# A causal convolution over eight sequences: its first sequence run ahead on its own, with idle products on TensorE and a causal matrix built without its zero columns

## The chip, the cores and the metric

The kernel runs on one core of a Trainium2 chip. The core has TensorE (PE in the profile, with its weight loads as PEld), VectorE (DVE), ScalarE (ACT), GpSimd (POOL) and SyncE (SP). Each of them takes its own instructions in order, and they wait for one another through semaphores. DMA transfers are issued from the queues of SP, ACT and POOL. The metric is the time of one execution on the device in microseconds; lower is better. A profiled execution has a time of its own, and within it a span from the first to the last instruction of the core.

## The reference

Four layers work on x of shape (8, 512, 128): a causal convolution, an FP4 feed-forward block, a test-time-training attention and a mixture of experts. Only the first is touched. For each of 8 sequences, with 16 heads of 8 channels and 31 taps, it computes:

```python
x = x + _L0_attn_ref(_layernorm(x, axis=-1), ...)

def _L0_attn_ref(x, W_pe, b_pe, stt_energy, W_fc, gamma, beta):
    residual = x
    avg = jnp.cumsum(x, axis=1) / jnp.arange(1, l + 1, dtype=x.dtype)[None, :, None]
    ci = avg.reshape(b, l, H, d).transpose(0, 2, 1, 3).reshape(b * H, l, d)
    pc = ci @ W_pe + b_pe
    dyn, gate = (pc[..., :K], pc[..., K:])
    energy = stt + jax.nn.sigmoid(gate) * dyn
    w = jax.nn.softmax(energy, axis=-1)
    ...
    for kk in range(K):
        out = out + w[:, :, kk:kk + 1] * padded[:, kk:kk + l, :]
    ...
    v = conv_loc @ W_fc.T + residual
    v = (v - mu) / jnp.sqrt(var + EPS) * gamma + beta
    return v
```

So each position needs the running mean of the normalised input, a gate and a tap value for each of 31 offsets, a softmax over the offsets, the weighted sum of the 31 last means, a projection and a second normalisation.

## The kernel before

`sequence_conv` holds the layer. It keeps channels in the 128 partitions and the 512 positions in the free dimension; the 31 taps go in four groups g of eight (16 heads x 8 taps = 128 partitions). Before any sequence it prepares constants: `inv` (1/t along 512 columns, by an iota on POOL and a reciprocal on DVE, L174 and L175), the causal matrix `tri` (four selects of 128 x 512 from `inv` on POOL, L190), the block weights `wbig` (eight multiplications on POOL, L214, behind a memset at L210), the biases, and the transposed projection `wfc_t`.

A sequence b goes through these steps, each a small function:

- `norm0` and `scaled` (L274): statistics on DVE, a root, then four scalings on ACT that write `xn`. The root is a Sqrt on ACT for the first two sequences and a chain of 13 short DVE instructions (`rsqrt`, L85 to L93) for 2 to 4 and for 5 to 7.
- `means` (L285): four matrix products of `xn` with `tri`, a copy of the result to `avg` on ACT (L288), and on SP one transfer to DRAM (`far`, L291) and eight back (`base`, L294), which spread the shifted means over the partitions.
- `gates` and `taps` (L300): for each g one matrix product for the gate, a Tanh and a linear step on ACT (L309, L310), and one product for the tap. Both write the two buffers of the pool `ps_e`.
- `energy` (L325 to L331): two DVE instructions for each g; the second keeps the running maximum `top`.
- `turn_top`, `greatest` (L341), `turn_greatest`: transposes on TensorE, a maximum on DVE, a copy on ACT, transposes back. `less` (L351) subtracts the maximum.
- `weigh` (L362, L364): seven exponentials on ACT.
- `shared` (L402) and `product` (L411): the products of weights and shifted means, two channels of eight on POOL and six on DVE for g of 0 to 2, all eight on DVE for g = 3. `add_up` (L420) sums them on TensorE.
- `part_sums`, `sums`, `invert`, `turn_inverse`: the softmax's denominator, over TensorE, ACT (`dn`, L375; `rw`, L386; `rbs`, L393) and DVE (L384).
- `scale_down` (L427), `project` (L432, L433), `norm1`, `finish` (L451 to L456): scaling, projection plus residual into a single-buffered PSUM pool `ps_p`, second normalisation, and the addition to x. The root of `norm1` runs on POOL (L130 to L138), on DVE for the last sequence.
- `add_beta` (L460): one POOL instruction that adds beta to x.

The order on each engine is written out by hand: `vec`, `ten`, `act` and `gp` are `Line` objects that chain an instruction behind the one given to them before. What is not given to a `Line` is put in place by the framework's scheduler. The loop at L496 works on three sequences at once: the products of b, the energies of b+1 and the gates of b+2, with the projection of b-1. The code ahead of the loop (L463 to L495) brings sequences 0, 1 and 2 to that state together. After the loop the buffers of the later layers are cleared and their weights loaded, all queued on SP.

## Time and profile before

| What | us |
|---|---|
| Median of 4 runs (lowest to highest) | 1301.51 (1300.51 to 1302.74) |
| The profiled execution | 1304.43 |
| Its span | 1302.7 |
| Busy in the span: PE, DVE, POOL, ACT | 1106.8, 771.6, 743.3, 489.7 |
| Mean granted TensorE clock | 0.939 of full speed |
| First `avg` copy of the convolution (L288) | 17.57 to 18.16 |
| First `product` of sequences 0, 1, 2, 3 (L411) | 44.55, 70.11, 96.87, 123.21 |
| Last `product` of the stage (L411) | 236.25 |
| x of the last sequence done (L456) | 253.43 |

Times in the trace are counted from the start of the span. A line of a timeline gives the start, the time from there to the end, the engine, the line of the kernel, the operation, what it writes and reads with the shapes, how many instructions were put together, and in brackets how long the engine was idle before and what released it. A product of two float32 operands appears as two records on TensorE (x8 stands for four). In the convolution the first product of one sequence follows that of the one before by about 26.3 us.

### The profile page before, as it was taken

The numbers are of one execution on the slowest core, as the hardware profiler recorded it, in microseconds if no ns is written. First come the engines' busy times: TensorE is split into PE (matmuls) and PEld (weight loads), VectorE is DVE, ScalarE is ACT, GpSimd is POOL, SyncE is SP. The second block draws the span as 40 slices with busy tenths as digits, with TensorE's granted clock in tenths as the row PEclk, the third lists the DMA queues.
The fourth block names the chain that finished last, engine by engine and source line by source line (L and its number), as shares of the span: only waits on it lengthen the run. The fifth ranks groups of instructions, "written<-read, shape, count | busy, mean of one in ns | idle before, by whom it ended". The sixth has DMA issues, their size and how long they took to land.

```text
span 1302.7 us, 15384 instructions
## 1 busy us (share of the span) xinstructions
PE 1106.8 (85%) x5219; PEld 659.6 (51%) x5219; DVE 771.6 (59%) x1769; ACT 489.7 (38%) x1001; POOL 743.3 (57%) x724
## 2 busy tenths in 40 slices
PE   5899997357877899999989999999899775499992
PEld 2343432135656445555565554555666444387772
DVE  7899999788985544444454444444556556033254
ACT  4556545166556422222243222222433122234331
POOL 4357656545554878888804887888103344355453
PEclk9899999878998899999999999999999886699997
DMA  5224327750000000000000000000000010212267
GB/s 157 77 77 124 106 77 238 278 172 1 1 1 1 1 1 1 1 1 1 1 1 1 1 1 1 1 1 1 1 1 21 29 33 30 62 51 70 64 178 207
DMA packets 66894, 67.26 MB, mean 52 GB/s; under 512 B 6927, under 2 KB 48734, under 8 KB 66816
## 3 DMA queue, kind: packets, MB, share of 16 engines
q1 hardware_dynamic: 59296, 56.57, 14.8%
q0 software_dynamic: 4608, 8.43, 2.1%
q10 hardware_dynamic: 2912, 1.29, 0.4%
q8 instruction: 41, 0.67, 0.2%
q14 instruction: 37, 0.30, 0.1%
HBM read 40.00 MB, written 27.13 MB: 52 GB/s over the span
## 4 chain that ended last, share of the span: by engine, by line
issue 66%; PE 9%; DMA 2%; POOL 1%; SPq 1%; DVE 0%; POOLq 0%; ACT 0%; DVEq 0%
PE ph L1470 4%; PE po L1483 4%; POOL own L1497 1%; DMA w<-in_L_ffn_W 1%; POOL res L1497 1%; PE tp L1455 1%; DMA own<-ye,tok 1%; DMA y<-own 1%; DMA L_ffn_bg<-in_L_ffn_bg 0%; DMA xe<-rows 0%; SPq L653 0%; SPq L759 0%; SPq L59 0%; DVE xt L1458 0%; SPq L1444 0%
## 5 line engine op out<-in xcount | busy, mean ns | idle before, releaser
L1141 POOL TENSOR_TENSOR ds<-sw,s 128x512 f32<-128x512 f32 x64 | 81.7, 1276 | 89.0 <-DVE sw L1136 89.0
L1371 POOL DMA_INDIRECT rows<-xr,slot x64 | 62.6, 977 | 106.1 <-DVE rs L93 55.5
L1143 POOL TENSOR_TENSOR ds<-ds,s 128x512 f32<-128x512 f32 x64 | 110.2, 1722 | 5.0
L1134 ACT COPY b<-pb 128x512 f32<-128x512 f32 x64 | 37.5, 586 | 163.0 <-PE pb L1130 156.4
L1497 POOL DMA_INDIRECT res<-ye,xe x60 | 58.5, 974 | 68.0 <-DVE ye L1495 29.7
L1138 DVE TENSOR_TENSOR h<-sw,b 128x512 f32<-128x512 f32 x64 | 51.7, 808 | 73.0 <-ACT b L1134 72.6
L1473 ACT ACTIVATE ht<-ph,b 128x512 f32<-128x512 f32 (+2 forms) x100 | 56.2, 589 | 94.3 <-PE ph L1470 75.4
L402 POOL TENSOR_TENSOR pr<-base,en 128x512 f32<-128x512 f32 x48 | 72.7, 1544 | 32.4 <-ACT en L364 32.3
L1144 POOL TENSOR_TENSOR ds<-ds,b 128x512 f32<-128x512 f32 x64 | 82.5, 1289 | 5.0
L1142 POOL TENSOR_TENSOR ds<-sw,ds 128x512 f32<-128x512 f32 x64 | 82.4, 1288 | 5.0
L1166 PEld LDWEIGHTS pp<-proj,ht 128*128 128x128 f32 x512 | 67.1, 191 | 30.8 <-issue 29.4
L411 DVE TENSOR_TENSOR pr<-base,w 128x3072 f32<-128x3072 f32 x24 | 79.7, 3320 | 1.7 <-ACT w L362 1.7
L1483 PE MATMUL po<-w,ht 128*128 128x128 f32 (+1 forms) x640 | 77.6, 278 | 0.3 <-ACT ht L1473 0.3
L1470 PE MATMUL ph<-xt,w 128*128 128x512 f32 (+2 forms) x200 | 74.1, 516 | 3.4 <-DVE xt L1458 3.4
L1136 DVE TENSOR_TENSOR sw<-pa,s 128x512 f32<-128x512 f32 x64 | 44.3, 692 | 54.5 <-ACT s L1132 54.5
L1161 ACT COPY ht<-pt 128x512 f32<-128x512 f32 x64 | 37.5, 586 | 103.3 <-PE pt L1159 103.3
L1483 PEld LDWEIGHTS po<-w,ht 128*128 128x128 f32 (+1 forms) x640 | 74.1, 188 | 1.3 <-ACT ht L1473 0.5
L1176 PE MATMUL ph<-proj_t,dpt 128*128 128x512 f32 x128 | 71.7, 642 | 0.4 <-ACT dpt L1174 0.4
L1178 DVE TENSOR_TENSOR db<-ph,sw 128x512 f32<-128x512 f32 x64 | 44.2, 691 | 45.5 <-PE ph L1176 45.5
L420 PE MATMUL cv<-pr,sel 128*32 128x512 f32 x512 | 61.8, 611 | 9.7 <-DVE pr L411 9.2
L1128 PE MATMUL pa<-gate,kt 128*128 128x512 f32 x128 | 67.7, 611 | 2.5 <-ACT b L1134 2.4
L1166 PE MATMUL pp<-proj,ht 128*128 128x128 f32 x512 | 67.6, 275 | 0.0
(327 smaller groups left out, 2590.2 us busy)
## 6 DMA issues: line engine op xcount, KB each, us to landing
base<-far SPq DMA_DIRECT2D x64, 268.0 KB
rows<-empty SPq DMA_DIRECT2D x1, 5005.0 KB
res<-zero SPq DMA_DIRECT2D x1, 4096.0 KB
own<-zero SPq DMA_DIRECT2D x2, 2048.0 KB
w<-in_L_ffn_W SPq DMA_DIRECT2D x16, 256.0 KB
y<-res SPq DMA_DIRECT2D x16, 256.0 KB
xe<-rows SPq DMA_DIRECT2D x7, 585.0 KB
y<-own SPq DMA_DIRECT2D x12, 256.0 KB
```

The source lines that it names most:

```text
L402: gp(nc.gpsimd.tensor_tensor(pr[:, d, :], s["base"][:, d, at], s["en"][:, g, :], ALU.mult))
L411: vec(nc.vector.tensor_tensor(s["pr"][g][:, :nv, :], s["base"][:, :nv, at], w.to_broadcast([P, nv, L]), ALU.mult))
L1128: nc.tensor.matmul(pa, ki, gate, start=True, stop=True)
L1141: nc.gpsimd.tensor_tensor(ds, sw, s, ALU.mult)
L1142: nc.gpsimd.tensor_tensor(ds, sw, ds, ALU.subtract)
L1143: nc.gpsimd.tensor_tensor(ds, ds, s, ALU.add)
L1144: nc.gpsimd.tensor_tensor(ds, ds, b, ALU.mult)
L1166: nc.tensor.matmul(pp, ht[:, c * P : (c + 1) * P], proj[:, c, :], start=(c == 0), stop=(c == NF - 1))
L1176: nc.tensor.matmul(ph, dpt, proj_t, start=True, stop=True)
L1470: ten(nc.tensor.matmul(ph[:, :n], self.w1[:, e, c * P : (c + 1) * P], xt[:, :n], start=True, stop=True))
L1483: ten(nc.tensor.matmul(po[:m, i - lo, :], ht[:, c, (i - lo) * P : (i - lo) * P + m], self.w2[:, e, c, :], start=(c == 0), stop=(c == NF - ...
L1497: sc = nc.gpsimd.indirect_dma_start(out=(self.slots.own[own - 1] if own else self.slots.res)[:, :], out_offset=bass.IndirectOffsetOnAxis(a ...
```

## The change

Part of it is about constants. `inv` is made by TensorE: an iota of 128 x 4 and a reciprocal of that (`by_t`), four products with the identity that spread it over the columns, and a DVE copy from PSUM. Behind those four, TensorE gets 14 products of the identity with itself (`busy`), whose result nobody reads. The selects for `tri` take only the columns from j x 128 on (512, 384, 256 and 128). The `wbig` products, the copy to `by_k` and `half` move from POOL to DVE, `wbig` as s within g. A Sqrt of a constant is run early on ACT, and the loads of `wrep`, the biases and `wfc` get places in ACT's line.

The rest is about order. The roots of sequences 0 and 1 are taken one by one, and the later ones by `roots`, a generator of 14 DVE instructions of which the caller places each. Sequence 0's gates write four PSUM buffers of other pools (`ps_w` and `ps_c`), one gate and one tap by turns. Sequence 0 is brought up to its first products before sequence 1's means are formed; the loop's body for b = 0 is written out ahead of the loop with sequences 1 and 2 filled in, and the loop starts at 1. `add_beta` is now in POOL's line, behind `shared` of its sequence in the loop. The means of sequences 1 and 2 are accumulated in the pool `ps_p`. The lines of the matrix products for the means are the same as before.

```diff
+    BUSY = 14
...
+        act(nc.scalar.activation(warm, cx.eps[1e-5], AF.Sqrt))
...
         inv = wp.tile([P, L], F32, tag="inv", name="inv")
-        nc.gpsimd.iota(inv, [[1, L]], base=1, channel_multiplier=0, allow_small_or_imprecise_dtypes=True)
-        vec(nc.vector.reciprocal(inv, inv))
+        by_t = wp.tile([P, G], F32, tag="by_t", name="by_t")
+        nc.gpsimd.iota(by_t, [[P, G]], base=1, channel_multiplier=1, allow_small_or_imprecise_dtypes=True)
+        vec(nc.vector.reciprocal(by_t, by_t))
+        pi = ps_c.tile([P, G, P], F32, tag="c", name="pi")
+        for j in range(G):
+            ten(nc.tensor.matmul(
+                pi[:, j, :], by_t[:, j : j + 1].to_broadcast([P, P]), cx.ident, start=True, stop=True
+            ))
+        busy = ps_p.tile([P, P], F32, tag="p", name="busy")
+        for _ in range(BUSY):
+            ten(nc.tensor.matmul(busy, cx.ident, cx.ident, start=True, stop=True))
+        vec(nc.vector.tensor_copy(inv, flat(pi)))
...
+                gp(nc.gpsimd.affine_select(
+                    out=tri[:, j, j * P :], in_=inv[:, j * P :], pattern=[[1, L - j * P]], compare_op=ALU.is_ge,
+                    fill=0.0, base=0, channel_multiplier=-1,
+                ))
...
+        stats0(0, 1)
+        root(0)
+        offset(0, 1)
+        scaled(0)
+        vec(nc.vector.tensor_copy(by_k.rearrange("h k s g -> h s g k"), rows.rearrange("h s (g k) -> h s g k", k=KK)))
+        act(nc.scalar.dma_start(
+            out=bias.rearrange("p s g -> p (s g)"), in_=by_k.rearrange("h k s g -> h (k s g)")
+        ))
+        for g in range(NGR):
+            for s in (1, 0):
+                n = min(KK, KC - KK * g)
+                vec(nc.vector.tensor_tensor(
+                    wbig[:, s, g, :, :n],
...
+        stats0(1, 2)
+        root(1)
+        offset(1, 2)
+        act(nc.scalar.activation(warm, cx.eps[1e-5], AF.Tanh))
+        wfc = wp.tile([P, D], F32, tag="wfc", name="wfc")
+        act(nc.scalar.dma_start(out=wfc, in_=ins["L0_attn_W_fc"]))
...
         seq = {0: means(0)}
-        gates(seq[0], 0)
+        stats0(2, 3)
+        half = wp.tile([P, NGR], F32, tag="half", name="half")
+        vec(nc.vector.tensor_scalar(half, bias[:, 1, :], 0.5, None, ALU.mult))
+        stats0(3, 5)
+        cur = seq[0]
+        for g, place in enumerate(((ps_w, "w0"), (ps_w, "w1"), (ps_w, "w2"), (ps_c, "c"))):
+            gate(cur, g, place)
+            tap(cur, g)
+            energy(cur, g)
         scaled(1)
...
+        turn_top(cur)
+        steps = roots(2, 5)
+        for _ in range(5):
+            next(steps)
+        greatest(cur)
+        turn_greatest(cur)
+        for _ in steps:
+            pass
+        less(cur)
+        weigh(cur, 0, 1)
+        nxt = seq[1] = means(1, ps_p, "p")
+        values(nxt, 0)
+        weigh(cur, 1, NGR)
+
+        shared(cur)
+        product(cur, 0)
+        part_sums(cur)
+        sums(cur)
+        for g in (0, 1):
+            energy(nxt, g)
+        values(nxt, 1)
+        product(cur, 1)
+        scaled(2)
+        then = seq[2] = means(2, ps_p, "p")
+        add_up(cur, 0)
         for g in (2, 3):
-            energy(seq[0], g)
...
+            energy(nxt, g)
+        invert(cur)
+        turn_top(nxt)
+        gates(then, 0)
+        stats0(5, B)
+        greatest(nxt)
...
+        less(nxt)
+        weigh(nxt, 0, 1)
+        seq[3] = means(3)
+        weigh(nxt, 1, NGR)
+        for _ in roots(5, B):
+            pass
+        product(cur, 3)
+        add_up(cur, 3)
+        for b in range(1, B):
```

## The prediction

> **What bounds the kernel now.** I read first the page's busy shares in 40 slices (32.6 us each). They show where VectorE (DVE) sets the pace.

> ```profile
> PE   5899997357877899999989999999899775499992
> DVE  7899999788985544444454444444556556033254
> PEclk9899999878998899999999999999999886699997
> ```

> The conv stage is the first seven to eight slices. DVE stands at 9 there, except in the first two, and the granted clock dips in the second. Everything after slice 8 issues the same instructions in the same order in both kernels, so only the first 253 us can change.

> Then the busy time by windows (columns: window, its length, then PE, PEld, DVE, ACT, POOL busy with counts, clock, DMA share, GB/s):

> ```profile
> 10.00:20.00 10.00, 5.96 (x12) 3.01 (x12) 8.13 (x39) 4.23 (x8) 4.06 (x10) 1.00 0.18 57
> 20.00:30.00 10.00, 9.00 (x25) 3.85 (x25) 5.66 (x8) 6.87 (x14) 1.91 (x3) 1.00 0.78 215
> 40.00:50.00 10.00, 9.24 (x21) 3.38 (x20) 8.29 (x6) 7.76 (x13) 4.56 (x6) 0.78 0.25 73
> 90.00:100.00 10.00, 9.66 (x44) 3.56 (x36) 10.00 (x4) 6.87 (x11) 4.56 (x5) 1.00 0.13 40
> ```

> From 60 us on DVE is full; before that it is not. What can be won is how early the full stretch begins. Its marker is the first `product` (L411) of sequence 1, at 70.11 in the trace. The timeline of the start:

> ```profile
> 7.14 1.28 ACT L268 ACT_TABLE_LOAD   x1 [7.14 <-DVE mv L257]
> 9.00 3.60 DVE L270 SCALAR_TENSOR_TENSOR off<-mv,rs 128x8 f32<-128x8 f32 x1
> 9.64 2.94 POOL L214 TENSOR_TENSOR wbig<-wrep,mask_h 128x128 f32<-128x128 f32 x8
> 13.27 4.25 PE L285 MATMUL av<-tri,xn 128*128 128x512 f32 x8 [13.27 <-ACT xn L274]
> 17.57 0.59 ACT L288 COPY avg<-av 128x512 f32<-128x512 f32 x1 [1.77 <-PE av L285]
> 26.67 2.32 PE L285 MATMUL av<-tri,xn 128*128 128x512 f32 x8
> 27.91 0.75 DVE L331 SCALAR_TENSOR_TENSOR top<-en,bias,top 128x512 f32<-128x512 f32 x1
> 40.61 2.28 DVE L351 TENSOR_TENSOR en<-en,mb 128x2048 f32<-128x2048 f32 x1
> 44.55 3.36 DVE L411 TENSOR_TENSOR pr<-base,w 128x3072 f32<-128x3072 f32 x1 [1.67 <-ACT w L362]
> ```

> The 0.17 us `off` takes 3.60, ending as POOL's run of `wbig` ends. The first means take 4.25 on a cold TensorE, 2.32 later. Between the last `top` of sequence 0 (28.66) and its `less` (40.61) stand statistics and roots of later sequences and energies of sequence 1.

> **The change, step by step** (us from the span's start, after against before).

> *To the scaled input.* A 128x4 iota (0.10 as the small memsets to 0.55 as the 128x512 one; I take 0.15) and a reciprocal of 0.20 (L269) replace 0.55 and 3.35. Four products of 128 columns on a cold array, 4.25 x 128/1280 = 0.43 each, are done by 4.6. The copy to `inv` is bounded by 0.49 (L329) and 0.75 (L325); with 0.60 it ends at 5.2, `sel` and `fold` at 5.6. Tile 0 has landed by then: the load of beta, queued behind that transfer, is issued at 3.59. Statistics of one sequence 1.08 to 1.15, root 0.30 with its table loaded ahead (1.28 off the path), reciprocal 0.20, `off` 0.17: the scaling starts at 7.5 against 12.64 and ends at 9.15.

> `off` runs free only if POOL's four selects are over. They shrink from 2048 to 1280 columns, 2.30 x 1280/2048 = 1.44, from 5.2 to 6.7, before `off` at 7.3. [...]

> *The idle products.* 14 x 0.43 = 6.0 if cold throughout, from 4.4 to 10.4; if the clock rises some 4.5 us after PE's start, as it did between 13.27 and 18.3, they end near 8.9. The means then take 2.3 and end at 11.2, instead of about 12.3 for cold ones from 8.0. I count this 1.9 as nothing, because ACT's queue ends later: `bias` issue (0.60) to 9.75; the root of sequence 1 waits for its statistics, which stand on DVE behind the eight `wbig` products. These start at 7.75, after POOL's memset (0.94), and if `wrep` has landed. `wrep` is issued behind the table load, near 3.8; in the trace it took 3.0 from issue to landing, so 6.9. Eight at 0.17 to 0.36 (the L91 row and POOL's own); I take 0.22, so 1.8 to 9.5. Statistics to 10.7, root 0.30, Tanh table 1.28, `warm` 0.20, `wfc` issue 0.60: 13.3. All this queues ahead of the first `avg` copy, which ends at **13.9 against 18.16**. Without the ACT queue, cold means would make it end near 12.9.

> *Sequence 0 alone.* Eight gate and tap products at 0.86 (half of L300's 1.88 pairs, less the drain) run without waits, having buffers of their own: 13.95 to 20.8. The last gate ends about 21.4, energy and `top` 1.5: **22.95 against 28.66**. Transposes 0.66, `mx` 0.69 (behind five root steps of 0.205), copy 0.60, transposes 0.66; nine root steps beside them; `less` 2.28, exp 0.68: the first `product` at **29.25 against 44.55**.

> *What was only put off.* Between the two firsts DVE now does: three products 9.99 and one of 4.42; energies and tops of sequence 1 (0.75 + 0.49 + 6 x 0.75 = 5.74) and half of sequence 2 (2.74); reciprocal 0.56, `mx` 0.69, `less` 2.28; statistics of 5 to 7, 3.24; 14 root steps, 2.87. That is 32.5, less some 1.0 for the 0.08 by which neighbours overlap. Waits are added, since nothing of sequence 1 is ready: 0.9 for its first tap (avg copy behind `less` and two exps, then gate, tanh, tap), and 4.1 before energy 2 of sequence 1. This is queued on PE behind `part_sums` and `sums`: last exp 38.1, product 1.0, copy 0.6, sums 1.0, gate, tanh, tap. So 29.25 + 31.5 + 5.0 = 65.7 against 70.11: **-4.4**. Of 15.3 won at the first product, 10.9 are given back.

> *`add_beta` in POOL's line.* It moves right behind `shared`. [...]

> ```profile
> 114.92 1.28 POOL L460 TENSOR_TENSOR x<-x,L_attn_beta 128x512 f32<-128x512 f32 x1
> 115.00 1.75 DVE L331 SCALAR_TENSOR_TENSOR top<-en,bias,top 128x512 f32<-128x512 f32 x1
> 236.46 4.26 POOL L138 TENSOR_TENSOR rs<-rs,sq 128x4 f32<-128x4 f32 x1
> 242.50 1.51 ACT L451 ACTIVATE v<-pj,off,rs 128x128 f32<-128x128 f32 x4 [9.35 <-POOL off L445]
> ```

> Three stalls of 1.0 go. Bounds 0 to 3.0. From the end of one third product (139.47) to the next reciprocal (156.65) DVE's road is 17.2 with the stall, and the road over PE and ACT (gates, exps, L451, `dn`, sums) 17.0. The second takes over: **-0.3**.

> At the end the last `add_beta` (1.28) stands ahead of sequence 6's root chain on POOL, started at 233.53. Five of its 0.29 steps then fall behind the last product (the 4.26 above), so L451 starts 1.1 to 1.3 later, and `project` of sequence 7, at 244.06 right behind these four, already waits for that: **+1.1** (bounds 0 and 1.3).

> Removed zero columns of the means: the matmul at L286 already reads only these columns; 0. SP's spreads of sequences 0 and 1 go out with their `avg`, 4.3 earlier and about as before; landing in some 9.5, they are ahead of their products.

> Sum: -4.4 - 0.3 + 1.1 = **-3.6** on the profiled span, 1302.7 to 1299.1. The profiled execution took 1304.43, 2.9 more than the median of the runs; on that median 1301.51 - 3.6 = **1297.9**.

> **Rivals.**
> - *The clock falls (slower).* Sequence 0 alone leaves PE gaps of 2 to 3 us. For: after 3.75 us of idleness before 38.77 the next means took 3.04 and the clock of that window is 0.78. Against: no gap above reaches 3.5. At half clock the eight products cost 8 x 0.86 = 6.8 more and the two waits of sequence 1 two products each, 3.4: +10.2 - 3.6 = +6.6, **1308**. It decides once some 3.6 us of this are lost. [...]
> - *The first copy slips.* `wrep` shares the engines with the tile loads, which the trace shows until 12.2. If it lands at 10 the chain is 2.2 later: **1300.1**; at 12.2, 1302.3.
> - *The stalls were all on the path.* If PE's and ACT's road also shortens, -2.7 more: **1295.2**. For: the third to fourth sequence ran 25.33 where others ran 26.34. Against: the next one ran 26.34 again without a beta beside it.

> **Chances.** Forecast 0.48 (1295.5 to 1299.5), stalls 0.20, slipping copy 0.20, clock 0.12. Between them 1293.5 to 1302.5 holds 8 in 10. Measurement tells 0.2%, 2.6 us, from no change, so the line is 1298.9. Nine tenths of the forecast, the stalls and a fifth of the slips lie below: faster 0.67. Slower: the clock and a tenth of the slips, 0.14. Within: 0.19.

> **What would show it.** First `avg` copy ending near 13.9; means of 2.3 already over at 11.2, with ACT loading a table between; first `product` at 29.3; a DVE wait of some 4 before the fifth energy; first product of sequence 1 at 65.7; `top` rows without 1.75; the last L451 pair 1 us later against the last product. Wrong, if the clock in 20 to 40 is under 0.9, if the first product of sequence 1 stands above 68, or if the period stays under 26.

## The result, and the profile after

The changed kernel takes 1297.61 us (median of 42 runs, 1292.77 to 1305.2); the kernel before takes 1301.75 (63 runs, 1297.85 to 1306.36). The ratio is 0.9971, with a 95% interval of 0.9963 to 0.9979: 3.8 us faster on 1301.75 (the medians lie 4.1 apart), where 3.6 was forecast. The profiled execution of the changed kernel took 1296.49, with a span of 1294.8.

The time is the one forecast; the sum behind it is not what this execution shows. Two of the three conditions named as "wrong, if" came true in it. First the page's 40 slices (32.4 us each), rows for PE, DVE and the granted clock:

```profile
PE   7999996457876899999989999999899785499992
DVE  6899999788986544444455444444557556123254
PEclk8999999868999899999999999999999887699997
```

The first two slices of the clock read 8 and 9, not 9 and 8 as before. One caution on this row: it counts as full all that lies ahead of the first clock record, which begins at 17.04 before and at 6.53 after. The first means of before, at 13.27, took 4.25 where warm ones took 2.32, though the row says 1.00 there. So after the change TensorE is fast earlier (the first means, at 8.92, take 2.40), and the clock falls earlier too (at 13.36, where before it first falls at 37.52). The windows of the start say how much (columns as before: window, its length, busy time of PE, PEld, DVE, ACT and POOL, clock, DMA share, GB/s):

```profile
10.00:20.00 10.00, 7.18 (x14) 3.33 (x13) 6.54 (x41) 3.91 (x7) 0.40 (x1) 0.67 0.52 158
20.00:30.00 10.00, 6.42 (x20) 3.31 (x19) 7.60 (x22) 5.92 (x12) 0.15 (x2) 0.84 0.58 155
30.00:40.00 10.00, 9.21 (x19) 3.54 (x18) 7.52 (x6) 6.11 (x10) 2.71 (x3) 0.81 0.26 84
```

Before, these windows had clocks of 1.00, 1.00 and 0.88. The timeline of the same stretch (start, duration, engine, line, what is written from what, and in brackets the idle time before it and what ended it):

```profile
8.08 0.16 DVE L269 SCALAR_TENSOR_TENSOR off<-mv,rs 128x4 f32<-128x4 f32 x1
8.92 2.40 PE L332 MATMUL av<-tri,xn 128*128 128x512 f32 x8 [0.19 <-ACT xn L290]
9.03 1.67 DVE L305 TENSOR_TENSOR wbig<-wrep,mask_h 128x128 f32<-128x128 f32 x8 [0.63 <-DMA wrep<-in_L_attn_W_pe]
12.11 1.28 ACT L314 ACT_TABLE_LOAD   x1
13.51 0.57 ACT L335 COPY avg<-av 128x512 f32<-128x512 f32 x1
...
14.13 2.08 PE L347 MATMUL eg<-avg,wbig 128*128 128x512 f32 x2 [2.82 <-ACT avg L335]
16.00 1.91 PE L347 MATMUL ev<-avg,wbig 128*128 128x512 f32 x2
17.71 1.91 PE L347 MATMUL eg<-avg,wbig 128*128 128x512 f32 x2
...
23.24 1.02 PE L347 MATMUL ev<-avg,wbig 128*128 128x512 f32 x2
...
29.49 4.47 PE L332 MATMUL av<-tri,xn 128*128 128x512 f32 x8
32.78 3.35 DVE L465 TENSOR_TENSOR pr<-base,w 128x3072 f32<-128x3072 f32 x1 [0.76 <-ACT w L416]
```

Up to the first copy everything stands where the prediction put it: `off` takes 0.16 instead of 3.60, the first means run warm in 2.40 and end at 11.3, and ACT's queue holds the copy until 14.08 (13.9 was forecast). Then TensorE, idle for 2.82 us while it waits for that copy, starts the eight gate and tap products at half clock. They take 10.1 us instead of 6.9, the second means 4.47 instead of 2.3, and the first `product` of sequence 1 stands at 69.70, against 70.11 before and 65.7 forecast.

The marks of this execution, beside the forecast and a second profile of the same changed kernel (called `again` below, on another chip):

| mark, us from the span's start | before | forecast | after | again |
|---|---|---|---|---|
| first copy of means ends | 18.15 | 13.9 | 14.08 | 14.36 |
| first product, sequence 0 | 44.55 | 29.25 | 32.78 | 29.84 |
| first product, sequence 1 | 70.11 | 65.7 | 69.70 | 66.15 |
| first product, sequence 7 | 223.45 | 218.75 (both steps) | 221.34 | 217.84 |
| last product | 236.25 | | 235.84 | 231.98 |
| next stage begins | 253.53 | 249.9 (whole sum) | 252.90 | 251.07 |

In the first profile only 0.6 us of the 7.9 by which the spans differ lie in the stage that was changed; the rest, 1049.2 against 1041.9, lies in instructions that are the same in both kernels.

### The profile page after: what moved, and what is told of

It is laid out like the page before. It is cut to its first block, busy times and chain, and to the rows that moved or that the text cites. A ratio compares the mean times of both kernels' runs of the same rounds, so it can differ in the third digit from the quotient of the medians.

```text
span 1294.8 us, 15453 instructions
## 1 busy us (share of the span) xinstructions
PE 1106.0 (85%) x5255; PEld 660.3 (51%) x5255; DVE 764.4 (59%) x1782; ACT 489.6 (38%) x1003; POOL 736.3 (57%) x714
## 4 chain that ended last, share of the span: by engine, by line
issue 66%; PE 8%; DMA 3%; POOL 1%; SPq 1%; DVE 1%; POOLq 0%; DVEq 0%; ACT 0%
PE po L1572 4%; PE ph L1559 4%; DMA w<-in_L_ffn_W 1%; DMA y<-res 1%; POOL own L1586 1%; POOL res L1586 1%; DMA y<-own 1%; PE tp L1544 1%; DMA L_ffn_bg<-in_L_ffn_bg 0%; DVE x L1535 0%; SPq L742 0%; DMA xe<-rows 0%; SPq L848 0%; DMA res<-ye,xe 0%; DMA own<-ye,tok 0%
## 5 line engine op out<-in xcount | busy, mean ns | idle before, releaser
L1225 DVE TENSOR_TENSOR sw<-pa,s 128x512 f32<-128x512 f32 x64 | 44.3, 692 | 54.4 <-ACT s L1221 54.4
```

## The experiments

Each of the kernels below ran on a chip on which the kernel before ran too. On those chips the kernel before takes 1269 to 1271 us, not 1302, and nearly all of the difference lies far behind this stage: the 64 indirect DMAs there (groups by line; the last columns are busy time, mean ns, and the idle time before them) wait 106.1 us on the first chip and 73.8 on another. The first profile of before, then the second:

```profile
L1371 POOL DMA_INDIRECT rows<-xr,slot x64 | 62.6, 977 | 106.1 <-DVE rs L93 55.5
```

```profile
L1371 POOL DMA_INDIRECT rows<-xr,slot x64 | 62.8, 982 | 73.8 <-DVE rs L93 45.1
```

So times are compared as ratios, and marks up to 254 us directly. The ratios (with 95% intervals) and the marks of one profile each:

| kernel | ratio to before | copy ends | seq. 0 | seq. 1 | seq. 7 | last product | next stage |
|---|---|---|---|---|---|---|---|
| before_again | | 18.25 | 44.66 | 70.12 | 223.46 | 236.26 | 253.54 |
| before_beta | 0.9996 (0.9984 to 1.0007) | 18.27 | 43.36 | 68.35 | 221.96 | 236.29 | 253.36 |
| order_only | 0.9995 (0.9984 to 1.0006) | 18.22 | 33.75 | 70.06 | 221.60 | 235.92 | 252.98 |
| prologue | 0.9949 (0.9931 to 0.9967) | 14.36 | 41.12 | 66.69 | 220.38 | 235.74 | 253.90 |
| prologue_2 | 0.9969 (0.9958 to 0.9980) | 14.24 | 41.25 | 66.33 | 220.01 | 234.51 | 251.56 |
| again | 0.9965 (0.9952 to 0.9978) | 14.36 | 29.84 | 66.15 | 217.84 | 231.98 | 251.07 |
| hold | 0.9977 (0.9967 to 0.9987) | 14.19 | 29.93 | 66.23 | 217.92 | 233.28 | 250.34 |
| no_idle | 0.9969 (0.9957 to 0.9981) | 14.22 | 31.61 | 67.91 | 219.55 | 233.97 | 251.03 |
| early | 0.9977 (0.9967 to 0.9987) | 12.27 | 31.64 | 68.25 | 219.93 | 234.26 | 251.32 |
| tail | 0.9992 (0.9983 to 1.0001) | 14.27 | 32.11 | 68.53 | 220.19 | 232.98 | 251.45 |
| tail_beta | 0.9966 (0.9953 to 0.9979) | 14.27 | 31.45 | 67.76 | 219.45 | 232.26 | 249.84 |
| best | 0.9965 (0.9952 to 0.9978) | 13.52 | 29.00 | 66.45 | 218.15 | 230.95 | 249.45 |

**again.** The changed kernel, unchanged.

> The changed kernel once more, for a second profile. Theory A (the half clock at the start belongs to the new order: TensorE idles 2.8 us between the first means and the first gate product, so a later execution shows it too): granted clock under 0.9 over 10 to 40 us, eight gate and tap products in about 10 us, first product of sequence 1 at 68 to 70 us. Theory B (the profiled execution was unlucky, most have full clock there): clock 1.0, the eight products in 6.9, first product of sequence 1 at 65.7 as forecast. Time under both 1297.6, give or take 1.5.

Its clock is 1.00 from 10 to 20 us, the eight products take 7.1, and the first products of sequences 0 and 1 stand 0.6 and 0.45 behind the forecast. Theory B holds for this execution, A for the first. What tells them apart is a matter of tenths. In the first profile after, the clock is at half from 13.36 to 20.18 and from 27.01 to 33.84, two stretches of 6.83 us; in `again` from 26.16 to 29.57, 3.41 us. Windows of 3.41 us, or twice that, laid to these edges, of the first profile after:

```profile
9.95:13.36 3.41, 1.36 (x7) 0.85 (x5) 3.01 (x21) 1.55 (x2) 0.00 (x0) 1.00 0.67 193
13.36:20.18 6.82, 6.04 (x7) 2.53 (x8) 3.58 (x23) 2.54 (x6) 0.40 (x1) 0.50 0.46 144
23.60:27.01 3.41, 1.27 (x7) 0.56 (x5) 3.06 (x8) 2.84 (x7) 0.15 (x2) 1.00 0.61 161
27.01:33.84 6.83, 5.38 (x14) 3.24 (x12) 5.62 (x14) 2.03 (x3) 0.26 (x1) 0.50 0.00 0
```

and of the second profile, `again`:

```profile
9.09:12.51 3.42, 2.39 (x8) 1.44 (x8) 2.84 (x17) 1.54 (x5) 0.00 (x0) 1.00 0.80 224
12.51:15.92 3.41, 1.51 (x4) 0.79 (x5) 3.38 (x27) 2.18 (x4) 0.41 (x1) 1.00 0.32 105
22.75:26.16 3.41, 0.93 (x7) 0.72 (x8) 3.07 (x14) 1.63 (x5) 0.00 (x0) 1.00 0.91 254
26.16:29.57 3.41, 3.41 (x9) 1.77 (x8) 2.81 (x5) 0.46 (x1) 0.00 (x0) 0.50 0.00 1
```

**hold.** Idle products fill that gap (`HOLD` is 12).

```diff
         seq = {0: means(0)}
+        for _ in range(HOLD):
+            ten(nc.tensor.matmul(busy, cx.ident, cx.ident, start=True, stop=True))
```

> 12 more idle products of 128 columns (0.215 each at full clock, 2.6 us) behind the first means, so that TensorE is busy until the first averages are copied. Theory A: clock 1.0 from 10 to 24 us, eight products in 6.9 to 7.3 instead of 10.1, first product of sequence 0 at 29.3 to 30 instead of 32.8, of sequence 1 at 66 to 67; time 2 to 4 us under the changed kernel, 1294 to 1295.5. Theory B: no change, 1297.6, since the clock is full there anyway in most executions. Rival C (the start is paid back in waits of sequence 1): first product of sequence 0 earlier by 3, that of sequence 1 by under 1, time 1297.

The marks are theory A's: eight products in 7.0, sequence 1 at 66.23. The clock halves at 25.67 (the transposes; 0.83 over 20 to 30), and from 216.8 to 223.6, where sequence 7 takes 2.6 longer than before. Windows laid to the edge at 25.67 would by my estimate have stood badly for the gap: the one from 12.01 to 15.43 would hold 1.05 us of work without the idle products (from 14.38 on). With them PE is busy for 10.00 of the 10.00 us from 10 to 20. The time is not theory A's: 0.9977 is no better than the changed kernel's 0.9965 on the same chip.

**no_idle.**

```diff
-        busy = ps_p.tile([P, P], F32, tag="p", name="busy")
-        for _ in range(BUSY):
-            ten(nc.tensor.matmul(busy, cx.ident, cx.ident, start=True, stop=True))
```

> The 14 idle products left out. Theory A: the first means run cold, 4.3 instead of 2.4, end near 13.2, and the copy of the averages ends near 14.1 as before since ACT's queue ends at 13.5; the gap of TensorE shrinks from 2.8 to about 0.9, the clock rises during the eight products, and the first product of sequence 0 stands at 29.5 to 32; time 1295 to 1297.6, not slower. Theory D (the idle products earn what they were put in for): the copy and all behind it 1.9 later, time 1299.5.

The means end at 13.60 instead of 11.59 (`again`) and the copy at 14.22 all the same: as the prediction said, the 1.9 that the idle products save is hidden by ACT's queue. The ratio is that of the changed kernel (0.9969 against 0.9965); theory D falls. The 14 products earn nothing here.

**early.** The root of sequence 1 goes to VectorE, so that the table is loaded sooner.

```diff
+        act(nc.scalar.activation(warm, cx.eps[1e-5], AF.Tanh))
         stats0(1, 2)
-        root(1)
-        offset(1, 2)
-        act(nc.scalar.activation(warm, cx.eps[1e-5], AF.Tanh))
+        for _ in roots(1, 2):
+            pass
...
-        stats0(3, 5)
```

> The root of sequence 1 is taken on VectorE (13 steps of 0.2 in idle time) instead of ScalarE, so that the Tanh table is loaded from 9.9 to 11.2 and the first averages are copied when the means end; the statistics of sequences 3 and 4 stand behind the first two energies. Copy ends at 12.0 instead of 14.1, TensorE's gap 0.7 instead of 2.8. Theory A: clock 1.0, eight products in 7, first product of sequence 0 at 27 to 28 instead of 32.8, of sequence 1 at 64.5 to 66; time 1293 to 1295. Theory B: only the 2.1 of the copy, and part of it paid back in waits: 1296 to 1297. Rival C: time 1297.

The statistics of sequences 3 and 4 go behind the first two energies. The copy ends 2.1 earlier and nothing follows from it. The first tanh needs `half`, and I had put the 13 root steps and a set of statistics ahead of `half` on VectorE. In the timeline of `early`:

```profile
15.60 0.13 DVE L521 TENSOR_SCALAR half<-bias 128x4 f32<-128x4 f32 x1
15.84 0.69 ACT L355 ACTIVATE sg<-eg,half 128x512 f32<-128x512 f32 x1 [3.56 <-DVE half L521]
```

In `again` the first tanh starts at 15.57. The clock of `early` is at half from 25.21 to 32.04, two windows where `again` has one, and the first product of sequence 1 stands 2.1 later. The test does not tell the theories apart.

**before_again.**

> The kernel before once more, for a second profile, to see what of the stage's end is the phase of the clock. Theory A (the waits and the order set the marks up to the first product of sequence 7, the clock's phase sets the rest): first product of sequence 1 at 69.5 to 71, of sequence 7 at 223 to 225, the last product 12.8 to 14.5 later, the stage's end 250.5 to 255.5. Rival: the marks of the first 220 us differ from the first profile by over 2 us, so that a difference of 4 between two kernels says little.

The two profiles of before agree to 0.02 us at every mark behind 70 us, on two chips. As far as one pair of profiles can show it, a difference of half a microsecond is real where the clock falls at the same places. (In both the clock halves at 37.5 to 44.3 and 215.0 to 218.4; whether that is chance was not tried.)

**prologue, prologue_2, order_only.** The change taken apart. `prologue` has the new constants and first means, then the old order; `order_only` the old constants (as at L174 to L240 of before) and the new order. Both have `add_beta` in POOL's line.

```diff
 # prologue
-        stats0(2, 3)
...
+        gates(seq[0], 0)
         scaled(1)
+        taps(seq[0], 0)
+        stats0(2, 5)
+        for _ in roots(2, 5):
+            pass
```

> The new constants, idle products and first means, but then the order of before (sequence 0 and 1 interleaved, 14 instructions of statistics and roots between). Theory P (the gain at the first product of sequence 1 is the shorter prologue alone, and working on sequence 0 alone only moves waits): copy of the first averages at 14.1 to 14.4, first product of sequence 0 at 40 to 41, of sequence 1 at 66 to 67; ratio to before 0.9965 to 0.998. Theory O (the order earns the larger part): first product of sequence 1 at 68 to 70, ratio 0.9985 to 1.000.

> The constants and the statistics of sequences 0 and 1 as before, then the new order. Theory P: copy of the first averages near 18.2, first product of sequence 0 at 33.5 to 34.5, of sequence 1 at 69.5 to 70.5; ratio 0.999 to 1.0005 less what the betas give (0.0005 to 0.0015). Theory O: first product of sequence 1 at 66 to 68, ratio 0.9965 to 0.998.

> The new prologue with the order of before, once more: its clock was half from 14.7 to 18.1 in the first profile, which cost 1.7. Theory P (the order earns nothing): ratio 0.995 to 0.997, not above the changed kernel's 0.9971; with full clock at the start the first product of sequence 1 at 64.5 to 65.5 and of sequence 7 at 218 to 219. Theory O: ratio 0.998 or more.

Neither theory holds as I put it. Theory P's marks for sequence 1 came in `prologue` and `order_only` (66.69 and 70.06), but `prologue_2` missed them, at 66.33 and, for sequence 7, 220.01. The order alone is worth nothing in time (0.9995) and comes 1.7 later than `before_beta` at sequence 1, to be 0.4 ahead at sequence 7. But it carries what the prologue wins: from `order_only` to `again` the copy comes 3.86 earlier, sequence 1 3.91 and sequence 7 3.76. In the old order only half is carried: from `before_beta` to `prologue_2` 4.03 at the copy, 2.02 at sequence 1. (In all four the clock falls once, for 3.41 us, between the copy and sequence 1.) There, in the old order, the statistics and 13 root steps of sequences 2 to 4 stand ahead of the first energy on VectorE, and no longer hide in a wait. The first energy of `before_beta`, then of `prologue`:

```profile
21.59 0.75 DVE L325 SCALAR_TENSOR_TENSOR en<-ev,bias,sg 128x512 f32<-128x512 f32 x1 [2.71 <-ACT sg L309]
```

```profile
20.01 0.17 DVE L269 SCALAR_TENSOR_TENSOR off<-mv,rs 128x12 f32<-128x12 f32 x1
20.11 0.75 DVE L379 SCALAR_TENSOR_TENSOR en<-ev,bias,sg 128x512 f32<-128x512 f32 x1
```

Against `prologue_2` the new order is ahead at sequence 7 by 2.2 where its clock holds at the start (`again`) and behind by 1.3 where it does not (after). By the time, the prologue with the old order is as fast as the whole change (0.9949 and 0.9969 against 0.9971 and, in `again`, 0.9965).

**before_beta.** One line:

```diff
-            nc.gpsimd.tensor_tensor(x, x, beta.unsqueeze(1).to_broadcast([P, G, D]), ALU.add)
+            gp(nc.gpsimd.tensor_tensor(x, x, beta.unsqueeze(1).to_broadcast([P, G, D]), ALU.add))
```

> The kernel before with add_beta alone given a place in GpSimd's order. From the first product of sequence 1 to that of sequence 7 the kernel before takes 153.3. Forecast: three stalls go, the road over TensorE and ScalarE takes over, 153.0, and 1.1 later in the tail: ratio 1.000 to 1.0006. Rival S (the stalls were on the path): 150.6 to 151.7 as the changed kernel showed (151.6), ratio 0.998 to 0.999, if the tail gives nothing back. Rival Q (the changed kernel's shorter loop comes from its start, not from the betas): 153.0 to 153.3 and ratio 1.000.

From sequence 1 to 7 it takes 153.61 instead of 153.34: the three stalls of 1.75 are gone and nothing is won. VectorE is busy for 25.5 of a period of 26.34, where it was 25.8 before, so another road sets the period, as forecast. Part of the stall also comes back: beside POOL's `shared` another `top` now takes 1.46 (at 99.00, and in the next three periods). But 1.8 is won ahead of sequence 1. Without a place in the line the first three additions ran early, and beside the one at 35.95 a root step of 0.17 took 1.16, which is 1.0 of the 1.8.

**tail.** Idle products in the gaps of sequences 6 and 7; `idle(n)` issues n products of the identity with itself.

```diff
             product(cur, 2)
+            if not nxt:
+                idle(8)
             add_up(cur, 2)
...
             product(cur, 3)
+            if not nxt:
+                idle(8)
+            elif not then:
+                idle(16)
             add_up(cur, 3)
...
         scale_down(cur)
+        idle(4)
         project(cur)
```

> The changed kernel with idle products in TensorE's gaps at the end of the stage: 16 between the third and fourth adding-up of sequence 6 (idle 4.6 us there), 8 and 8 between those of sequence 7 (2.0 and 2.4), 4 ahead of the last projection. Theory A (those gaps let the clock fall just as sequence 7 needs TensorE): no half clock between 216 and 240, first to last product of sequence 7 in 12.8 instead of 14.1 to 15.4, the stage's end 15.5 to 17.0 after the last product; the whole 1.5 to 2.5 shorter than the changed kernel, ratio to before 0.995 to 0.996. Rival (DVE and GpSimd set the tail): first to last product over 14, ratio 0.997.

What it fills, in the profile after: TensorE is idle 4.61 us, comes back at half clock, and the reciprocal of sequence 7 waits 2.02 for it.

```profile
218.16:221.57 3.41, 0.10 (x4) 0.10 (x8) 3.41 (x2) 3.35 (x6) 2.92 (x1) 1.00 1.01 400
221.57:224.98 3.41, 3.41 (x20) 0.85 (x24) 3.12 (x1) 1.67 (x5) 3.41 (x3) 0.50 1.03 324
```

```profile
221.47 3.60 PE L474 MATMUL cv<-pr,sel 128*32 128x512 f32 x16 [4.61 <-DVE pr L465]
227.84 0.56 DVE L438 RECIPROCAL rs<-sm 128x64 f32<-128x64 f32 x1 [2.02 <-PE sm L434]
231.29 1.27 POOL L514 TENSOR_TENSOR x<-x,L_attn_beta 128x512 f32<-128x512 f32 x1
235.84 4.42 DVE L465 TENSOR_TENSOR pr<-base,en 128x4096 f32<-128x4096 f32 x1
241.80 1.50 ACT L505 ACTIVATE v<-pj,off,rs 128x128 f32<-128x128 f32 x4 [9.06 <-POOL off L499]
```

and the same stretch of `tail`:

```profile
220.31 1.92 PE L479 MATMUL cv<-pr,sel 128*32 128x512 f32 x16 [0.49 <-DVE pr L470]
224.98 0.56 DVE L443 RECIPROCAL rs<-sm 128x64 f32<-128x64 f32 x1 [0.86 <-PE sm L439]
230.07 1.27 POOL L519 TENSOR_TENSOR x<-x,L_attn_beta 128x512 f32<-128x512 f32 x1
232.98 4.42 DVE L470 TENSOR_TENSOR pr<-base,en 128x4096 f32<-128x4096 f32 x1
240.37 1.50 ACT L510 ACTIVATE v<-pj,off,rs 128x128 f32<-128x128 f32 x4 [10.48 <-POOL off L504]
```

Sequence 7 takes 12.79 from first to last product, as in before (12.80), instead of 14.50: theory A. But the gain is spent at once. The four scalings by ACT start 7.39 after the last product, against 5.96 after and 6.25 before, and the stage ends 18.5 behind it, not 17.1. That is `add_beta` ahead of the root chain on POOL. The forecast of 15.5 to 17.0 missed this. The time was missed too: 0.9992 is behind the changed kernel's 0.9971, and the intervals do not meet.

**tail_beta.** As `tail`, with the last `add_beta` moved up by most of a sequence:

```diff
-            add_beta(b)
+            if nxt:
+                add_beta(b)
             add_up(cur, 1)
             if old:
                 norm1(old, nc.gpsimd)
+            if nxt and not then:
+                add_beta(B - 1)
```

> As tail, with the last add_beta taken out from ahead of sequence 6's root chain on GpSimd: it stands behind the chain of sequence 5, where GpSimd waits 2 us for the exps. Theory A (the forecast's +1.1 is real, and was hidden in the changed kernel by the colder clock, which made VectorE late): four shifts of sequence 6 start 6.0 to 6.3 after the last product instead of 7.4, the stage ends 17.0 to 17.4 after the last product instead of 18.5; first to last product of sequence 7 stays at 12.8. Rival (the road over the last product, the sums and the projection sets it anyway): 18.5. The whole time follows only as far as the later clock lets it: ratio 0.9955 to 0.9985.

```profile
232.26 4.42 DVE L470 TENSOR_TENSOR pr<-base,en 128x4096 f32<-128x4096 f32 x1
238.81 1.51 ACT L510 ACTIVATE v<-pj,off,rs 128x128 f32<-128x128 f32 x4 [9.64 <-POOL off L504]
```

The scalings start 6.55 behind the last product and the stage ends 17.58 behind it: 0.8 and 0.9 of the 1.1 come back, not quite what was expected. The road over the last product does not set it; POOL does. In the time it is 0.9966 against 0.9992, some 3.3 us, of which the next stage's mark shows 1.6 (249.84 against 251.45); why `tail` as a whole was so slow stays open.

**best.** `tail`, with a start meant to be shorter: bias table sent ahead of the first statistics, statistics and root of sequence 1 ahead of `wbig`, later statistics and root steps moved back, idle products around the transposes.

> As tail, and at the start: the bias table is sent ahead of the first statistics (its DMA takes 5.0 us to land and the first tanh waits for it), statistics and root of sequence 1 stand ahead of the eight wbig products so that the Tanh table is loaded by 11.6, and 9 and 5 idle products keep TensorE busy ahead of the two groups of transposes. Theory A (the start's shift is carried whole in this order, and the clock is the rest): first copy ends at 12.2 instead of 14.1 to 14.4, first product of sequence 0 at 27 to 28, of sequence 1 at 62.5 to 64.5 instead of 66.15 at best, of sequence 7 at 214.5 to 216; ratio to before 0.992 to 0.994. Rival C (paid back in waits of sequence 1): first product of sequence 1 at 65.5 to 66.5, ratio as tail.

The start failed on a transfer that I had not looked up. The copy that builds the bias table now stands ahead of the first statistics and waits for `rows`:

```profile
7.66 0.43 DVE L299 COPY by_k<-rows 16x96 f32<-16x96 f32 x1 [1.98 <-DMA rows<-in_L_attn_stt_energy]
```

So the scaling starts 1.1 later and the copy ends only 0.84 earlier. The clock stays full to 30.0 and then falls on the gates of sequence 1: its first product stands 37.45 behind that of sequence 0, where `again` has 36.31. The stage ends at 249.45, the earliest of all, 4.1 ahead of before, and the ratio is still that of the changed kernel.

## Why the prediction came out right

*The first copy, 13.9.* Right (14.08 and 14.36), and for the reason given: ACT's queue, ending 13.5. `wrep` landed near 9.0, not at 6.9, which made the statistics of sequence 1 about 1 us late; the issue of `wfc`, counted at 0.60 behind the table load, went out ahead of it and gave half of that back.

*The idle products, counted as nothing.* Right: `no_idle` has the same copy and the same ratio.

*The eight products of 0.86 at full clock, and with them the -4.4 at sequence 1.* This is the step that failed in the profiled execution. The prediction weighed the clock rival against gaps of "3.5" and gave it 0.12. No run shows 3.5 us as a limit: the gap of 2.82 in the first profile stood ahead of half clock, with 1.36 us of work in the window that held most of it; the gap of 2.81 in `again` did not, with 2.39 and 1.51 in the two windows that it touches. Among the six profiles whose start has this gap, the clock fell in four (after, prologue, `tail`, `tail_beta`; in the three of these with the new order the first product of sequence 0 stands at 32.78, 32.11 and 31.45, in `again` at 29.84) and held in two. The first product of sequence 1 in the four that have the new order too stands at 69.70, 68.53, 67.76 and 66.15, on average 68.0. So the term is -2.1 on average, with -4.0 as its best case. The rival's price was too high: it put 10.2 on it, and the first profile lost 3.6 at sequence 1 against the second. Slow second means, which the sum does not have, show in both profiles of the changed kernel: 4.47 and 3.83 instead of 2.3, after the windows with 1.27 and 0.93 us of work.

Where the clock holds, the chain of terms is right: from first product to first product 36.31 in `again`, 36.45 forecast. Of the waits, 0.9 was 1.04 and 4.1 was 2.59; a `top` that took 1.81 beside POOL's products, which I had not seen coming, makes up for most of it.

*`add_beta` in the loop, -0.3.* Right in kind: the stalls go and the other road takes over. Before, the tops at 88.67, 115.00 and 141.35 took 1.75 beside the additions of beta at 88.59, 114.92 and 141.27, where the `top` at 167.68 took 0.75; by what, no trace shows. Of these rows of the profile after, the first is the `top` that stood at 115.00.

```profile
112.92 0.75 DVE L385 SCALAR_TENSOR_TENSOR top<-en,bias,top 128x512 f32<-128x512 f32 x1
124.76 1.44 DVE L385 SCALAR_TENSOR_TENSOR top<-en,bias,top 128x512 f32<-128x512 f32 x1
126.94 1.06 PE L434 MATMUL sm<-fold,dn 128*128 128x16 f32 x8 [0.82 <-ACT dn L429]
```

The second row shows that another `top`, beside POOL's `shared`, takes 1.44 now, as in `before_beta`; the third is TensorE waiting for ACT on the other road. As a size the term missed. The stretch from sequence 1 to 7 is 151.5 to 151.7 in every kernel with the new order against 153.3 before: -1.65. `before_beta` shows that the betas give none of this; with the new order the first two periods are 24.85 and 25.58 (`again`; VectorE is busy for 24.7 and 24.9 of them), before 26.34 sets in.

*The last `add_beta`, +1.1.* Right, but not visible in the profile after, where the scalings even start 0.3 earlier against the last product. There VectorE was late by 1.7 (the clock was 0.50 from 221.57 to 224.98), so that POOL's chain got one step further than before ahead of the last product: its step at 235.96 took 4.35 beside that product of 4.42, with five steps to come instead of six. With the clock held, `tail` shows +1.14.

*The sum.* At best clock it was -4.0, -1.65, then +1.3 in sequence 7 and +1.8 behind it, both with the clock at half (`again`: from 217.3 and from 237.8): -2.5 at the end of the stage, against -0.6 in the first profile. The runs say -3.8. The missing 1.3 to 3.2 us do not show in the stage of these two profiles, and are not explained. So it is in part luck that the forecast of -3.6 was met: its largest term came out at -2.1 to -4.0 instead of -4.4, its second at -1.65 instead of -0.3, and some of the measured gain has no term in the sum. Which part of the change earns the time is clearer: the new constants do so with either order (0.9949 and 0.9969 with the old), and neither the order without them (0.9995) nor the betas alone (0.9996) do. Behind the stage, over the profiles on the later chips, the remaining time goes from 1010.1 (`early`) to 1016.0 (`best`) with the same instructions; `before_again` has 1015.6 and `again` 1012.0. Over the 44 recorded executions of the changed kernel the span follows the mean granted clock (correlation -0.90, 0.64 us for each 0.001). So some of the -3.8 may be luck in where the clock falls later, or the change may shift those odds; no run here separates the two. In the profiles this is why `best`, which ends the stage 1.6 earlier than `again`, is not faster as a whole. No version tried is clearly ahead of the changed kernel.

## What to carry to other kernels

A shift won at the start is worth what the queues behind it carry: here the same shorter prologue was carried whole in one order and by half in the other, because of statistics that had hidden in a wait. When a serial stretch leaves TensorE waiting, lay windows to the edges that the clock has in the trace and count TensorE's busy time in them, instead of looking at the length of gaps alone: here one gap of 2.8 us had half clock behind it and another had not. Fill the gap with idle products where something waits for TensorE next. That settled the marks here (`hold`, `tail`), but no run shows a gain in the whole time from it. A term that a profile does not show (the +1.1) may be covered by another loss: take that loss away before calling the term wrong.

## What the runs showed of the hardware

The clock of TensorE in the two profiles of before and after, counted over windows of 3.41 us laid to the edges of its records, from the first record (17.04 and 6.53) to 1200 us. PE's ends are modelled, and some of its records may be missing.

| window | PE busy in it, us | windows | followed by the other clock |
|---|---|---|---|
| at full clock | under 1.3 | 21 | 21 |
| at full clock | 1.3 to 1.7 | 10 | 5 |
| at full clock | over 1.7 | 586 | 0 |
| at half clock | under 2.7 | 46 | 0 |
| at half clock | 2.7 to 3.0 | 6 | 2 |
| at half clock | over 3.0 | 24 | 24 |

The stretches at half clock last from 3.41 us (215.01 to 218.43 before) over 6.83 (13.36 to 20.18 after) to 37.55 (before, from 1092.2), and their edges stand elsewhere in the two. This is what two executions show; what lies behind it, no run shows.
